# A selective-scan image: which groups take their scan input from VectorE, and how the softplus of a projection is placed

## The chip, the cores and the metric

The kernel runs on one core of one Trainium2 chip. The time is the device time of the program in microseconds (us), the median of several executions. The profile is one execution taken by the hardware profiler. Names used below: PE is TensorE's matrix engine (PEld its weight loads), DVE is VectorE, ACT is ScalarE, POOL is GpSimd, SP is the queue that issues almost all transfers. L564 means line 564 of the kernel before.

## The reference

The input is four images of 384 channels and 32x32 positions. A group normalisation is followed by a selective scan in four directions, a layer norm and a gelu; then causal attention and a mixture of four experts (two used per token). What the change touches is the scan of the first image:

```python
dts = einsum('bkrl,kdr->bkdl', dts, dt_projs_weight)       # rank 12 -> 384 channels
dt = softplus(dts + dt_projs_bias)                          # k = 4 directions
def step(h, inp):
    dtt, ut, bt, ct = inp
    dA = exp(dtt[..., None] * A)                            # A: 16 states per channel
    h = h * dA + (dtt * ut)[..., None] * bt[:, :, None, :]  # the scan, over 1024 positions
    y = einsum('bkdn,bkn->bkd', h, ct)
```

For each image, direction, channel and state there is one linear recurrence over 1024 positions. Its two inputs are the decay `exp(dt * A)`, called `da`, and `v = (dt * u) * B`.

## The kernel before

**Units and groups.** A unit is one [128 x 1024] tile: 32 channels times 4 states on the partitions, 1024 positions along each. There are 768 units, 192 for each image. Four units that share a state quarter `q` and take four channel blocks `j` form a group; one group shares one tile of broadcast B and C rows. The first image has 48 groups, numbered 0 to 47 below. `EACH` is 16 units (one direction k and channel third m), `IMAGE` is 192 units.

**Ticks.** Instructions are issued by hand in a loop over ticks, one tick `t` per unit, and every engine executes its own instructions in that order. Tick `t` issues, in this order: `decay(t+2)` (the exponential `da`, L551, ACT), the multiplication `v = du * B` of unit t (`front`, L558, DVE) unless the unit's v was made another way, `turned(t+1)` (below), the product with C of unit t-1 (`back`, L571, POOL), the scan of unit t (`middle`, L564, DVE), and in the second tick of a group the sum over states of the group before (`row`, L596, PE: eight matmuls, recorded as sixteen). After these come one step of the preparation and the steps of the generators in a list called `side`. A `yield "wait", n` ends a generator's share of this tick and lets it go on n ticks later.

**The second way to v.** In the first image a generator, `feed`, makes v for some groups without DVE. It transposes the rows of `dt * u` on PE into a PSUM bank (L796, two times four 128x128 transposes for a group), multiplies them there by B with 32 ACT instructions of 128x128 (L819, eight in a tick, each eight followed by a wait), and leaves the result in a tile `st`. Then `turned(n)` (L841) transposes eight 128x128 blocks of `st` back, straight into the PSUM tile v of unit n. There are two `st` tiles. A fill may begin when the last but one group begun has been scanned; one that would begin too late (later than `n0 - AHEAD`, with `AHEAD` = 5 ticks) is left out, and the group keeps its DVE multiplication. A group whose v comes this way is called a turned group below, the others plain groups. The loop takes every odd `q`: groups 1, 3, 5 and so on, of which group 1 is left out.

**Buffers.** The PSUM tile v has two buffers, `da` three, h seven. During the first image two PSUM banks are shared by everything else: the projections (`pxd`, L391; `pdt`, L424), the group normalisation, and the transposes of `feed`. A bank is free again when ACT has read it.

**The projections of dt.** `project_dt` runs once for each image, pair of directions and channel third. For each half h of the positions it takes both banks, issues two matmuls (L424), waits a tick, and issues two softplus on ACT (L430). The exponential and the softplus need different ACT tables, so a table load stands before the softplus and another before the next `da`. Ten such projections are issued before tick 192: five of image 0 and five of image 1. The first one of all is made apart (`first_dt`).

Of the kernel before, what the change touches and what calls it, by code (L numbers as in the profile page):

```python
# [33 lines left out]
NQ = N // NI  # L34
NJ = P // DJ
# [7 lines left out]
AHEAD = 5  # L43
# [6 lines left out]
def hybrid_kernel(  # L50
# [60 lines left out]
    clock = [-100]  # L111
# [180 lines left out]
    def columns(v):  # L292

        return v.rearrange("p (h w) -> p w h", w=HW)
# [113 lines left out]
    def project_dt(b, pair, m, u, xd):  # L408

        ks = PAIRS[pair]  # L410
        while not slots.ready(3 + pair):
            yield "wait", 1
        v = u[m]
        if pair == 1:
            v = slots.now(f"ut_{b}_{m}", P, L)
            nc.scalar.copy(v.rearrange("p (w h) -> p w h", h=HW), columns(u[m]))
        dts = [slots.now(f"dt_{b}_{k}_{m}", P, L) for k in ks]
        for h in range(NH):
            while not banks.ready(2):
                yield "wait", 1  # L420
            pss = [banks.now(f"pdt_{b}_{k}_{m}_{h}") for k in ks]
            for i, k in enumerate(ks):
                r = slice(64 * pair + 32 * i, 64 * pair + 32 * i + R)
                nc.tensor.matmul(  # L424
                    pss[i], wdt[r, m * P : (m + 1) * P], xd[r, bass.ts(h, 512)],
                    start=True, stop=True,
                )
            yield "wait", 1
            for i, k in enumerate(ks):
                nc.scalar.activation(  # L430
                    dts[i][:, bass.ts(h, 512)], pss[i], AF.Softplus, bias=dtb[:, k, m : m + 1]
                )
                banks.give(f"pdt_{b}_{k}_{m}_{h}")
        yield "wait", 1
        for i, k in enumerate(ks):
            nc.sync.dma_start(dts_d[b, k][0, m * P : (m + 1) * P, :], dts[i])
            du = yield from slots.take(f"du_{b}_{k}_{m}", P, L)
            nc.vector.tensor_mul(du, dts[i], v)  # L438
            yield "wait", 1
            nc.sync.dma_start(dts_d[b, k][1, m * P : (m + 1) * P, :], du)  # L440
            if b == 0:
                stored_du.add((k, m))
            slots.give(f"dt_{b}_{k}_{m}", f"du_{b}_{k}_{m}")
        if pair == 1:
            slots.give(f"ut_{b}_{m}")

    EACH = NQ * NJ
    IMAGE = M * K * EACH
# [31 lines left out]
    def preparation(b):  # L480

        u = first_x if b == 0 else load_image(b)
        yield "wait", 3
        yield from groupnorm(b, u)
        while clock[0] < IMAGE * (b - 1) + 24:

            yield "wait", 1
        xd = one.tile([P, L], F32, tag="xd", name=f"xd_{b}")
        if b == 0:
            nc.scalar.activation(dump, eps, AF.Softplus)  # L490
            scan_weights()
        yield from project_x(b, 0, u, xd)
        if b == 0:
            fetch(-3, ("bc",))
            first_dt(u, xd)
            yield "start", 0
        yield from project_x(b, 1, u, xd)
        for m in range(M):
            for pair in range(2):
                if b > 0 or m > 0 or pair > 0:  # L500
                    yield from project_dt(b, pair, m, u, xd)
                yield "wait", 0 if b == 0 and m == 0 else 12
# [254 lines left out]
    def feed():  # L757
        bt = one.tile([P, 2, NT, 4 * N], F32, tag="fx0", name="bt")

        def turn_rows(pair):  # L760
            while pair not in stored_rows:
                yield "wait", 1
            rows = yield from slots.take(f"bt_{pair}", 4 * N, L)
            nc.sync.dma_start(rows, rows_d[0, pair].rearrange("k j n l -> (k j n) l"))
            yield "wait", 2
            ps = yield from banks.take(f"pbt_{pair}")
            for t in range(NT):
                nc.tensor.transpose(
                    ps[:, t * 4 * N : (t + 1) * 4 * N], rows[:, t * P : (t + 1) * P],
                    ident[: 4 * N, : 4 * N],  # L770
                )
            yield "wait", 1
            nc.scalar.copy(bt[:, pair], ps.rearrange("p (t n) -> p t n", t=NT))
            banks.give(f"pbt_{pair}")
            slots.give(f"bt_{pair}")

        begun = []
        yield from turn_rows(0)
        for n in range(0, IMAGE, EACH):
            u = units[n]  # L780
            if clock[0] > n + EACH - NJ - AHEAD:
                continue
            if u["pair"] == 1 and u["m"] == 0 and u["i"] == 0:
                yield from turn_rows(1)
            while (u["k"], u["m"]) not in stored_du:
                yield "wait", 1
            name = f"turn_{u['name']}"
            du = yield from slots.take(name, P, L)
            nc.sync.dma_start(du, dts_d[0, u["k"]][1, u["m"] * P : (u["m"] + 1) * P, :])
            yield "wait", 2  # L790

            def dut(q, h, du=du, name=name):
                ps = banks.now(f"{name}_{q}_{h}")
                for t in range(4):
                    o = (4 * h + t) * P
                    nc.tensor.transpose(ps[:, t * P : (t + 1) * P], du[:, o : o + P], ident)  # L796
                return ps

            for q in range(1, NQ, 2):
                n0 = n + q * NJ  # L800
                if clock[0] > n0 - AHEAD:
                    continue
                while len(begun) >= 2 and clock[0] < begun[-2] + NJ:

                    yield "wait", 1
                if clock[0] > n0 - AHEAD:
                    continue
                begun.append(n0)
                st = pools["st"].tile([P, NT, NJ * P], F32, tag="st", name=f"st_{n0}")
                ps = [None, None]  # L810
                for h in range(2):
                    if ps[h] is None:
                        while not banks.ready():
                            yield "wait", 1
                        ps[h] = dut(q, h)
                        yield "wait", 1
                    for t in range(4):
                        for i in range(NI):
                            nc.scalar.activation(  # L819
                                st[:, 4 * h + t, :].rearrange("p (d i) -> p i d", i=NI)[:, i, :],  # L820
                                ps[h][:, t * P : (t + 1) * P], AF.Copy,
                                scale=bt[:, u["pair"], 4 * h + t, u["i"] * 2 * N + q * NI + i :][:, :1],
                            )
                        if t == 1:
                            if h == 0 and banks.ready():
                                ps[1] = dut(q, 1)
                            yield "wait", 1
                    banks.give(f"{name}_{q}_{h}")
                    yield "wait", 1
                scaled[n0] = st  # L830
            slots.give(name)
# [477 lines left out]
    clock[0] = -2  # L1309
    side.append(later())  # L1310
    side.append(feed())
    decay(0)
    decay(1)
# [85 lines left out]
```

## Time and profile before

| | |
|---|---|
| time, median of three runs | 3795.2 us (3794.46 to 3797.17) |
| profiled execution: its time, its span | 3795.0 us, 3793.2 us |
| first image: first scan of image 0 to first scan of image 1 | 49.0 to 680.7 us |
| DVE multiplications for v (L558), all images | 678, mean 1241 ns |
| ACT multiplications by B (L819) | 736, mean 532 ns |
| transposes back to v (L841) | 720, mean 364 ns |
| table loads at the exponential (L551) | 108, mean 1283 ns |
| granted TensorE clock, mean over the span | 0.927 |

The busy times of the profile count instructions from start to end, and consecutive small instructions of one engine overlap, so the mean of 532 ns is not the pace of L819: the timeline, which merges a run of equal instructions, gives the pace. A wait is shown as the idle time ahead of an instruction with the engine and line that ended it.

### The profile page before, as it was taken

The numbers are of one execution on the slowest core, as the hardware profiler recorded it, in microseconds if no ns is written. First come the engines' busy times: TensorE is split into PE (matmuls) and PEld (weight loads), VectorE is DVE, ScalarE is ACT, GpSimd is POOL, SyncE is SP. The second block draws the span as 40 slices with busy tenths as digits, with TensorE's granted clock in tenths as the row PEclk, the third lists the DMA queues.
The fourth block names the chain that finished last, engine by engine and source line by source line (L and its number), as shares of the span: only waits on it lengthen the run. The fifth ranks groups of instructions, "written<-read, shape, count | busy, mean of one in ns | idle before, by whom it ended". The sixth has DMA issues, their size and how long they took to land.

```text
span 3793.2 us, 34275 instructions
## 1 busy us (share of the span) xinstructions
PE 3366.5 (89%) x11543; PEld 1518.3 (40%) x11543; DVE 2964.4 (78%) x2084; ACT 2089.9 (55%) x2767; POOL 1815.1 (48%) x776
## 2 busy tenths in 40 slices
PE   4666666689999999799999999889999999999999
PEld 1333333245333334345333343354343434644444
DVE  6899899998889999989998999999999982210000
ACT  5888888555656656556655555455554552422121
POOL 2777777554455556445555565455665550000000
PEclk7767877799999999898999999899999999999999
DMA  6655655635576767336666565345656551222321
GB/s 207 218 209 219 220 199 208 230 122 184 191 245 208 255 205 251 140 136 225 215 221 223 197 212 185 143 167 195 215 194 237 180 182 38 91 78 80 96 83 53
DMA packets 407983, 678.80 MB, mean 179 GB/s; under 512 B 33488, under 2 KB 280576, under 8 KB 407808
## 3 DMA queue, kind: packets, MB, share of 16 engines
q1 hardware_dynamic: 401600, 676.22, 52.0%
q8 instruction: 91, 1.49, 0.2%
q10 hardware_dynamic: 6208, 0.39, 0.1%
q14 instruction: 84, 0.69, 0.1%
HBM read 604.57 MB, written 71.96 MB: 178 GB/s over the span
## 4 chain that ended last, share of the span: by engine, by line
DVE 42%; PE 40%; ACT 7%; issue 6%; DMA 3%; POOL 1%; DVEq 0%; SPq 0%; POOLq 0%; ACTq 0%
DVE h L564 25%; PE ph L1182 13%; PE fy L1207 13%; DVE v L558 12%; PE y L596 4%; ACT da L551 2%; PE ss L925 2%; PE pq L896 2%; PE pv L907 2%; PE v L841 1%; PE pxd L391 1%; ACT st L819 1%; DVE du L438 1%; DMA du<-dts 1%; PE po L991 1%
## 5 line engine op out<-in xcount | busy, mean ns | idle before, releaser
L571 POOL TENSOR_TENSOR h<-h,bc 128x1024 f32<-128x1024 f32 x768 | 1814.0, 2366 | 1308.6 <-DVE v L558 1142.8
L564 DVE TENSOR_TENSOR_SCAN h<-da,v 128x1024 f32<-128x1024 f32 x768 | 1750.5, 2284 | 104.4 <-PE v L841 29.7
L551 ACT ACTIVATE da<-dt,a 128x1024 f32<-128x1024 f32 x768 | 883.3, 1156 | 923.7 <-DVE h L564 887.2
L1182 PE MATMUL ph<-fx,w 128*128 128x512 f32 x2304 | 1024.8, 601 | 6.5 <-ACT dt L430 2.3
L1207 PE MATMUL fy<-ht,w 128*128 128x512 f32 x2304 | 1021.2, 600 | 1.5 <-ACT dt L430 0.9
L558 DVE TENSOR_TENSOR v<-du,bc 128x1024 f32<-128x1024 f32 x678 | 841.7, 1241 | 38.8 <-DMA du<-dts 21.7
L1182 PEld LDWEIGHTS ph<-fx,w 128*128 128x128 f32 x2304 | 434.9, 192 | 583.4 <-issue 528.9
L1207 PEld LDWEIGHTS fy<-ht,w 128*128 128x128 f32 x2304 | 436.8, 192 | 574.9 <-issue 552.2
L596 PE MATMUL y<-h,sel 128*32 128x512 f32 x3072 | 493.8, 661 | 101.4 <-POOL h L571 101.3
L1167 ACT ACTIVATE ht<-ph,b1s 128x512 f32<-128x512 f32 x384 | 257.2, 678 | 459.5 <-PE ph L1182 459.1
L1216 DVE SCALAR_TENSOR_TENSOR fy<-fy,b2s,tw 128x512 f32<-128x512 f32 x96 | 72.4, 754 | 425.8 <-PE fy L1207 425.8
L596 PEld LDWEIGHTS y<-h,sel 128*32 128x32 f32 x3072 | 97.4, 116 | 412.2 <-issue 219.8
L841 PE MATMUL v<-ident,st 128*128 128x128 f32 x720 | 143.1, 364 | 110.6 <-DVE h L564 110.6
L819 ACT ACTIVATE st<-turn,bt 128x128 f32<-128x128 f32 x736 | 213.6, 532 | 0.1
L841 PEld LDWEIGHTS v<-ident,st 128*128 128x128 f32 x720 | 115.4, 189 | 155.6 <-DVE h L564 78.3
L1171 ACT ACTIVATE ht<-ht 128x3072 f32<-128x3072 f32 x64 | 176.9, 2763 | 0.8
L551 ACT ACT_TABLE_LOAD x108 | 138.6, 1283 | 13.8 <-DMA dt<-dts 11.9
L991 PE MATMUL po<-pt,vt 128*128 128x256 f32 x480 | 105.4, 368 | 9.4 <-ACT pt L887 9.4
L424 PE MATMUL pdt<-xd,wdt 12*128 12x512 f32 x184 | 81.0, 762 | 34.8 <-ACT dt L430 19.4
L925 PE MATMUL ss<-axn,qt 128*128 128x512 f32 (+3 forms) x288 | 106.1, 514 | 0.8 <-ACT pr L943 0.5
L991 PEld LDWEIGHTS po<-pt,vt 128*128 128x128 f32 x480 | 93.1, 195 | 24.9 <-ACT pt L887 12.0
L939 DVE TENSOR_REDUCE nb<-ss 128x1 f32<-128x512 f32 (+3 forms) x48 | 26.1, 554 | 78.8 <-PE ss L930 63.5
(200 smaller groups left out, 1661.7 us busy)
## 6 DMA issues: line engine op xcount, KB each, us to landing
bc<-rows SPq DMA_DIRECT2D x384, 512.0 KB, 4.9
w<-in_w SPq DMA_DIRECT2D x384, 384.0 KB, 6.1
dt<-dts SPq DMA_DIRECT2D x192, 512.0 KB, 3.8
du<-dts SPq DMA_DIRECT2D x192, 512.0 KB, 6.7
dts<-dt SPq DMA_DIRECT2D x48, 512.0 KB, 5.3
dts<-du SPq DMA_DIRECT2D x48, 512.0 KB, 3.8
fx<-t2d SPq DMA_DIRECT2D x12, 768.0 KB, 5.3
tw<-mkd SPq DMA_DIRECT2D x32, 256.0 KB, 6.3
```

The source lines that it names most:

```text
L551: nc.scalar.activation(u["da"], spread["dt4", n], AF.Exp, scale=a4[:, g, u["q"] : u["q"] + 1])
L558: return nc.vector.tensor_tensor(u["v"], spread["du4", n], spread["bc", n][:, 0, :], ALU.mult)
L564: nc.vector.tensor_tensor_scan(u["h"][:, ::step], u["da"][:, ::step], u["v"][:, ::step], 0.0, op0=ALU.mult, op1=ALU.add,)
L571: product = nc.gpsimd.tensor_tensor(h, h, spread["bc", n][:, 1, :], ALU.mult)
L596: nc.tensor.matmul(y, sel, h, start=first, stop=last, tile_position=(0, jj * DJ))
L819: nc.scalar.activation(st[:, 4 * h + t, :].rearrange("p (d i) -> p i d", i=NI)[:, i, :], ps[h][:, t * P : (t + 1) * P], AF.Copy, scale=bt[ ...
L841: nc.tensor.transpose(u["v"][:, t * P : (t + 1) * P], st[:, t, u["j"] * P : (u["j"] + 1) * P], ident)
L925: nc.tensor.matmul(ps[:, : e - o], qt[:, c, i * P : (i + 1) * P], xn[:, c, o:e], start=(c == 0), stop=(c == M - 1 and e <= i * P),)
L991: nc.tensor.matmul(pv[:, o:], vt[:, j, m * P : (m + 1) * P], pts[step][j // 4][:, j % 4, o:], start=False, stop=(j == nj - 1),)
L1167: nc.scalar.activation(ht[:, f, :], ps, AF.Identity, bias=bias)
L1182: nc.tensor.matmul(ps, tiles[n][:, c, (f % 2) * P : (f % 2 + 1) * P], xns[h][:, c, :], start=(c == 0), stop=(c == M - 1),)
L1207: nc.tensor.matmul(pss[m], tiles[n][:, f, :], hts[fh][:, f, :], start=(fh == 0 and f == 0), stop=(fh == 1 and f == FH - 1),)
```

## The change

Two edits. In `project_dt` the tick between the matmuls and the softplus stays for the first half, and goes for the second half while the first image is being scanned: the four softplus of one projection then follow each other in one tick, with the second pair of matmuls between the two pairs of softplus. In `feed` the choice of groups changes from every odd `q` to the groups whose number modulo five is 1, 3 or 4. The rule on late fills and the number of `st` tiles are the same.

```diff
@@ project_dt
             for i, k in enumerate(ks):
                 r = slice(64 * pair + 32 * i, 64 * pair + 32 * i + R)
                 nc.tensor.matmul(
                     pss[i], wdt[r, m * P : (m + 1) * P], xd[r, bass.ts(h, 512)],
                     start=True, stop=True,
                 )
-            yield "wait", 1
+            if h == 0 or clock[0] >= IMAGE:
+
+                yield "wait", 1
             for i, k in enumerate(ks):
                 nc.scalar.activation(
                     dts[i][:, bass.ts(h, 512)], pss[i], AF.Softplus, bias=dtb[:, k, m : m + 1]
                 )
@@ feed
-            for q in range(1, NQ, 2):
+            for q in range(NQ):
                 n0 = n + q * NJ
-                if clock[0] > n0 - AHEAD:
+                if n0 // NJ % 5 not in (1, 3, 4) or clock[0] > n0 - AHEAD:
                     continue
                 while len(begun) >= 2 and clock[0] < begun[-2] + NJ:
 
                     yield "wait", 1
```

In the program that results, 26 groups of the first image are turned: 3, 6, 8, 9, 11, 13, 14, 16, 18, 19, 21, 23, 24, 26, 28, 29, 31, 33, 34, 36, 38, 39, 41, 43, 44 and 46. Before, 23 were: 3 (three of its four units), 5, 7, and every odd group up to 47. The counts of the two programs:

| instruction | before | after |
|---|---|---|
| L558, DVE multiplication for v | 678 | 664 |
| L819, ACT multiplication by B | 736 | 832 |
| L796, transposes of dt * u | 184 | 208 |
| L841, transposes back to v | 720 | 832 |
| table loads at L430 and at L551 | 46 and 108 | 36 and 97 |

SP issues the same number of transfers. From the layer norm of image 1 on, PE has the same instructions in the same order; between tick 192 and there, the preparation of the next images stands a tick or a few earlier.

## The prediction

> **What bounds the kernel now.** I first read the table by stage. Its columns are: the stretch and its length, then busy time of PE, PEld, DVE, ACT and POOL, each with its number of instructions, then the granted TensorE clock, the DMA share and GB/s.
>
> ```profile
> 97.00:216.00 119.00, 77.51 (x347) 36.33 (x345) 108.09 (x59) 98.04 (x214) 85.24 (x36) 0.74 0.59 213
> 216.00:448.00 232.00, 146.92 (x723) 76.11 (x723) 214.29 (x126) 198.67 (x412) 171.81 (x72) 0.76 0.60 219
> 448.00:681.00 233.00, 146.86 (x675) 72.75 (x674) 217.23 (x119) 182.84 (x363) 171.90 (x73) 0.72 0.58 212
> 681.00:1900.00 1219.00, 1121.30 (x3972) 503.21 (x3973) 1121.13 (x811) 737.11 (x819) 652.45 (x277) 0.94 0.58 200
> ```
>
> The first three rows are the first image, the only place that the change edits. DVE is busy 92% there (540 of 584 us), PE 64%, POOL 73%. ACT's 82% overstates it (below). Next I asked the waits between 96 and 680 us who is late:
>
> ```profile
> DVE h L564 <- PE v L841: 29.7, 21, 3.8
> ...
> ACT da L551 <- DVE h L564: 101.1, 82, 3.6
> ```
>
> Columns: total us, times, longest. DVE waits for practically one thing, the transposes that make v in turned groups, 29.7 us. ACT waits 101.1 us for scans to free a `da` buffer: it runs ahead of DVE and is not the limit. Third, DVE's timeline around a clean turned group (15):
>
> ```profile
> 250.54 2.29 DVE L564 TENSOR_TENSOR_SCAN h<-da,v 128x1024 f32<-128x1024 f32 x1
> 252.75 1.29 DVE L558 TENSOR_TENSOR v<-du,bc 128x1024 f32<-128x1024 f32 x1
> 254.17 8.91 DVE L564 TENSOR_TENSOR_SCAN h<-da,v 128x1024 f32<-128x1024 f32 x4
> 263.98 2.29 DVE L564 TENSOR_TENSOR_SCAN h<-da,v 128x1024 f32<-128x1024 f32 x1 [0.91 <-PE v L841]
> ```
>
> A plain unit steps 254.17 - 250.54 = 3.63 us from scan to scan; over all 75 such steps between 97 and 681 us the mean is 3.66. A turned unit without a wait steps 2.20 us. The last unit of the group waits 0.91 us. PE shows why:
>
> ```profile
> 258.69 1.97 PE L841 MATMUL v<-ident,st 128*128 128x128 f32 x8 [0.21 <-DVE h L564]
> 260.59 2.24 PE L596 MATMUL y<-h,sel 128*32 128x512 f32 x16
> 262.75 1.09 PE L841 MATMUL v<-ident,st 128*128 128x128 f32 x8
> ```
>
> With two v buffers the transposes of a unit can start when the scan two units earlier has ended; in the second tick the row (2.24 us) stands between them, and the next v is late.
>
> **Removed: 14 multiplications on DVE.** 678 - 664 = 14 at L558. Each takes its step from 3.66 to 2.20 us: 14 x 1.46 = 20.4 us, all of it on the path, since DVE sets the pace.
>
> **Added on ACT: 3 fills, hidden.** 96 more instructions at L819. Their pace is in ACT's timeline:
>
> ```profile
> 402.43 1.18 ACT L551 ACTIVATE da<-dt,a 128x1024 f32<-128x1024 f32 x1
> 403.45 2.34 ACT L819 ACTIVATE st<-turn,bt 128x128 f32<-128x128 f32 x8
> 405.46 1.24 ACT L551 ACTIVATE da<-dt,a 128x1024 f32<-128x1024 f32 x1
> ```
>
> Eight of them take 405.46 - 403.45 = 2.0 us of the queue, a fill 8.0, three fills 24 us. A tick with eight costs ACT 3.03 us (402.43 to 405.46), less than a plain DVE step, more than a turned one. Before, fills mostly fall into plain groups; now each second group of a pair (9, 14, 19, 24, 29, 34, 39, 44) has the eights in its ticks 1 to 3, where ACT loses 3 x (3.03 - 2.20) = 2.5 us. Its cover is the lead: `da` of unit n+2 starts when scan n-1 ends, takes 1.15, and is wanted two scans (4.4 us) later, a lead of 3.25 us; a plain group, where ACT gains 0.6 to 2.5 us a tick, follows each time. So 0 us; if the cover is gone, up to 2.5 us for each of these eight groups. Here the Trainium skill speaks against the change: "ScalarE: Activation LUTs", section "Rules for kernel authors", puts multiplications on VectorE, as the faster engine for them (its factor is for bf16; all is fp32 here). By the work it is right even here: a unit's v costs ACT 2.0 us (and PE a transpose back) against 1.46 us on DVE. If ACT were the limit, the change would be worth 24 us of fills against the table loads below, about nothing. The row with 101.1 us of ACT waiting decides: I count DVE's side.
>
> **Taken away on ACT: 21 table loads, hidden.** ACT's timeline at a projection:
>
> ```profile
> 419.27 1.28 ACT L430 ACT_TABLE_LOAD   x1
> 420.57 1.26 ACT L430 ACTIVATE dt<-pdt,dtb 128x512 f32<-128x512 f32 x2
> 421.85 1.28 ACT L551 ACT_TABLE_LOAD   x1
> 423.14 1.15 ACT L551 ACTIVATE da<-dt,a 128x1024 f32<-128x1024 f32 x1
> ```
>
> 21 x 1.28 = 27 us, so ACT as a whole is 3 us better off. The skill's page just named, section "What ACT_TABLE_LOAD costs", sets 2.66 us for a switch, a drain of 1.38 included, which would make 56 us; the rows show the next instruction 0.01 to 0.02 us after the load's end, so 1.28 it is. On the path it is worth nothing except through PE, which stands at the second `pdt` until ACT has read the first bank; that wait stays, because the second matmuls still need the banks of the first softplus. New is that ACT waits for them: two short matmuls, of which one lies under a softplus, some 0.5 us in 10 projections, covered by the lead. The four softplus with their loads last 1.28 + 4 x 0.6 + 0.5 + 1.28 = 5.5 us; the lead (3.25) plus one scan (2.2) just covers this in a turned group, and easily in a plain one (7.3 for two steps).
>
> **Added on PE: 112 + 24 transposes, and where they stand.** A further turned unit brings eight transposes (1.04 to 1.97 us over 66 such runs), a tick has 2.20, so they fit as they do now. The transposes of dt * u come in fours, 0.60 to 1.12 us (34 blocks). Before, these stand in plain groups nearly always; in the eight second groups of a pair the fours now stand in ticks 0 and 1. In tick 0 there is room. In tick 1 the four stand behind the row and ahead of the last unit's v: that wait grows by 0.60 to 1.12 us. I take 1.12, as PE is often at the slow pace here (clock 0.72 to 0.76): 8 x 1.12 = 9.0 us.
>
> **Stalls, before and after.** Of the 29.7 us, groups that meet a projection or a normalisation hold most: group 3 has 2.5, group 7 5.2, group 27 6.7, group 33 2.2, group 41 2.1, together 18.7. The other 18 hold 11.0, 0.6 each. Group 27 is the one where a `pxd` waited for a bank that ACT still read, with v behind it:
>
> ```profile
> 411.93 2.84 PE L391 MATMUL pxd<-x,wx 128*128 128x512 f32 x6 [2.38 <-ACT bc L400]
> ...
> 415.78 2.29 DVE L564 TENSOR_TENSOR_SCAN h<-da,v 128x1024 f32<-128x1024 f32 x1 [3.81 <-PE v L841]
> ```
>
> I laid the new order against the ticks. The softplus now fall at ticks 5, 11, 28, 44, 62, 109, 129, 147, 167 and 183. Of these only tick 44 has turned units right behind it (group 11): v of unit 46 waits behind the second `pdt` (ACT: decay 1.05, load 1.28, first softplus 0.6 after scan 43), the transposes for the next fill (which want the bank of the third softplus) and its own eight; about 7 us after scan 43, against two scans of 2.2: 2.5 us, and 1.7 for the row and the second four, 4.2 in all. Group 3 I put at 1.5, group 24 (normalisation) at 1.5, group 26 (`pxd` beside its first units) at 2.0. The other 22 have 0.6 each. After: 22 x 0.6 + 9.0 + 4.2 + 1.5 + 1.5 + 2.0 = 31.4 us, against 29.7: +1.7.
>
> POOL takes 2.37 us a product against 2.20 of a turned step and so falls behind 0.17 a unit, 1.4 over a pair; the waits just counted (0.6 and 1.7) give that back.
>
> **After the first image.** DVE and PE are both at 92% there, and their work is the same but for a few ticks' shift of the preparation, so the gain arrives whole. I allow 3 us either way.
>
> **Sum.** -20.4 + 1.7 = -18.7 us. On the profiled execution (span 3793.2, with 1.8 us around it, 3795.0) that is 3776.3; the median is 0.2 us above that execution, so about 3777 us.
>
> **Rivals.** (1) Half is eaten: the fours wait for banks, or `da` comes late in second groups, up to 2.5 us in most of eight. Then -18.7 + 8 x 1.6 = about -6, 3789. For it: in the waits of before PE already stands 13.5 us at `pdt` for softplus. Against it: a fill takes a bank only when ACT's reads of it stand ahead, and the fill before ended three ticks or so earlier. (2) More than I count: fewer loads also clear the stalls beyond 0.6 that I left in groups 3, 11, 24 and 26 (6.8 us), and the fours run at 0.60 (8 x 0.52 = 4.2 us less): -18.7 - 11.0 = about -30, 3766. For it: the two worst stalls of before (groups 7 and 27) stand beside loads. (3) Slower: in each pair PE's queue head waits for ACT in a turned group, as at 415.78 us, so that one more stall of 3.8 us falls into each of eight pairs: 8 x 3.8 = 30 against 18.7, +12, 3807. It decides from 18.7 / 8 = 2.3 us a pair on. For it: second groups now join fill, row and return transposes on PE. Against it: in ticks 0 and 1 of these groups the banks are free and ACT has its lead. (4) The count is as told by the program itself, so a change without effect is not to be had; but if PE, not DVE, bound the image, the step would stay at 3 us and the time at 3795. PE's 64% and the merged scans of 8.91 us speak against it.
>
> **How the numbers follow.** The likeliest, with its own range of -11 to -25 (3770 to 3784), gets 0.60; rival 1 0.17, rival 2 0.12, rival 3 0.06, rival 4 0.05. A difference under 0.2% (7.6 us) can't be told from none. Faster by more: 0.60 + 0.12 + a third of rival 1 = 0.78. Within: 0.16. Slower: 0.06. The range leaves out the far end of rival 2 and rival 3: 3765 to 3793.
>
> **What would show it.** In the profile after: L558 664 times; the turned step still 2.20; DVE waits for v 28 to 35 us in the first image, with 1.5 to 2 us ahead of the last unit of each second group and about 4 us in group 11; ACT still waiting for scans, at 70 to 110 us; the first scan of image 1 at about 662 us. I am wrong if DVE waits for `da`, if waits in second groups pass 2.3 us beyond those of the others, or if what the first image gains is lost after it.

## The result and the profile after

The changed kernel takes 3787.36 us, the median of 15 runs (3783.72 to 3791.61), against 3795.2 us (3789.45 to 3803.41) for the kernel before, run beside it. The ratio is 0.998, with a 95% interval of 0.9973 to 0.9988. It is faster by 7.8 us where 18.7 were forecast. 3787 lies inside the range (3765 to 3793), but outside the likeliest case's own (3770 to 3784); the number nearest to it is that of the first rival, 3789. A later repeat of the changed kernel (`e11_changed_again`) gave 6.4 us (3790.7 against 3797.12). The profiled execution took 3788.9 us with a span of 3787.2, which is 6.0 less than before.

In the changed kernel, and in all others that keep both edits without new lines above them, the lines behind the first edit stand two lower: the scan is L566, the multiplication L560, `da` L553, the fill L821, the transposes L843, `du` L440, softplus L432.

The page's groups, after (busy us, mean ns of one, then the idle time before them and what ended most of it):

```profile
L566 DVE TENSOR_TENSOR_SCAN h<-da,v 128x1024 f32<-128x1024 f32 x768 | 1749.4, 2284 | 97.6 <-PE v L843 19.8
...
L560 DVE TENSOR_TENSOR v<-du,bc 128x1024 f32<-128x1024 f32 x664 | 825.8, 1244 | 37.2 <-DMA du<-dts 20.2
```

There are 664 multiplications, so the 14 are gone. The table by stage, after, with the same columns as before; the last row ends at the first scan of image 1:

```profile
97.60:221.40 123.80, 82.05 (x370) 39.52 (x370) 112.99 (x62) 93.97 (x207) 86.43 (x37) 0.72 0.63 219
221.40:446.00 224.60, 154.83 (x790) 83.62 (x790) 202.89 (x114) 197.51 (x455) 170.70 (x72) 0.75 0.60 216
446.00:676.50 230.50, 149.69 (x715) 72.62 (x714) 217.62 (x115) 184.83 (x408) 172.47 (x73) 0.76 0.61 223
```

From unit 12 to the first scan of image 1 the image now lasts 578.9 us (583.8 before) and DVE is still busy for 533.5 of them, 92% again. The first scan of image 1 starts at 676.5 us, against 680.7 before and 662 forecast. So most of the gain is missing already inside the first image. The waits of DVE there (60 to 681 us; total, times, longest), after:

```profile
DVE h L566 <- PE v L843: 19.8, 26, 2.4
DVE du L440 <- ACT dt L432: 7.5, 9, 2.0
DVE v L560 <- DMA du<-dts: 5.1, 4, 2.5
```

and those of ACT (49 to 681 us), after:

```profile
ACT da L553 <- DVE h L566: 85.8, 64, 3.7
ACT dt L432 <- PE pdt L424: 19.2, 11, 3.2
```

The wait for the transposes fell from 29.7 to 19.8 us, where I had it rise to 31.4. The second row of DVE has no counterpart before: the multiplication `du = dt * u` (L440, twice for each projection, in the ticks behind the softplus) never waited then. Beside it stands ACT's: the second pair of softplus waits 19.2 us for its matmuls; before, ACT waited 1.1 us for `pdt`.

A book of DVE's time, from the first scan of image 0 to the first scan of image 1, taken from the two traces instruction by instruction (busy time without overlap, us):

| | before | after | difference |
|---|---|---|---|
| length | 631.7 | 626.2 | -5.5 |
| multiplications for v (102, 88), busy | 123.0 | 108.4 | -14.6 |
| idle before multiplications for v | 3.2 | 6.8 | +3.6 |
| scans, busy | 433.3 | 432.1 | -1.2 |
| idle before scans | 44.9 | 33.4 | -11.5 |
| `du` (20), busy | 23.5 | 30.0 | +6.5 |
| idle before `du` | 0 | 7.5 | +7.5 |
| one operation of the normalisation, stretched | 0.5 | 2.7 | +2.2 |
| idle before the normalisation | 0 | 2.1 | +2.1 |

This is one execution of each; in the trace of the repeat the same stretch is 629.1 us long, 2.6 less than before. The 14.0 us at `du` are the largest loss. The timeline after, around the projection at unit 109, shows where it comes from:

```profile
413.05 2.07 PE L424 MATMUL pdt<-xd,wdt 12*128 12x512 f32 x2 [5.02 <-ACT st L821]
...
414.97 1.28 ACT L432 ACT_TABLE_LOAD   x1
415.05 3.64 PE L598 MATMUL y<-h,sel 128*32 128x512 f32 x16
...
416.27 1.27 ACT L432 ACTIVATE dt<-pdt,dtb 128x512 f32<-128x512 f32 x2
...
418.62 2.08 PE L424 MATMUL pdt<-xd,wdt 12*128 12x512 f32 x4
420.73 1.27 ACT L432 ACTIVATE dt<-pdt,dtb 128x512 f32<-128x512 f32 x2 [3.19 <-PE pdt L424]
421.45 1.23 DVE L440 TENSOR_TENSOR du<-dt,x 128x1024 f32<-128x1024 f32 x1 [1.99 <-ACT dt L432]
...
422.02 1.28 ACT L553 ACT_TABLE_LOAD   x1
...
423.31 1.15 ACT L553 ACTIVATE da<-dt,a 128x1024 f32<-128x1024 f32 x1
```

Between the softplus of the first half and those of the second ACT stands 3.19 us: PE has the row sum in its queue (3.64 us), then the second matmuls (2.08 us). From the first load to the next `da` it is 8.3 us instead of the 5.5 in my sum. In six of the ten projections there is no row in between, and the stop is the matmuls alone, 1.58 us, as at unit 44:

```profile
209.63 1.27 ACT L432 ACTIVATE dt<-pdt,dtb 128x512 f32<-128x512 f32 x2 [1.58 <-PE pdt L424]
```

The first line at unit 109 shows a second new wait: a matmul of the first half stands 5.02 us at the head of PE's queue until ACT has read a fill's transposes from the bank that it wants, so the row behind it starts late. Over the first image (60 to 681 us), after:

```profile
PE pdt L424 <- ACT st L821: 16.4, 5, 5.1
```

Before, this wait was 4.5 us, in two times.

### The profile page after: what moved, and what is told of

Read it like the earlier page. It is cut to its first block, busy times and chain, and to the rows that moved or that the text cites. A ratio compares the mean times of both kernels' runs of the same rounds, so it can differ in the third digit from the quotient of the medians.

```text
span 3787.2 us, 34585 instructions
## 1 busy us (share of the span) xinstructions
PE 3382.9 (89%) x11679; PEld 1527.3 (40%) x11679; DVE 2961.2 (78%) x2070; ACT 2085.0 (55%) x2841; POOL 1816.6 (48%) x776
## 4 chain that ended last, share of the span: by engine, by line
DVE 42%; PE 38%; ACT 8%; issue 6%; DMA 3%; POOL 1%; SPq 1%; DVEq 0%; POOLq 0%; ACTq 0%
DVE h L566 25%; PE ph L1184 13%; DVE v L560 13%; PE fy L1209 12%; PE y L598 3%; ACT da L553 2%; PE pq L898 2%; PE pv L909 2%; ACT st L821 2%; POOL h L573 1%; PE pxd L391 1%; PE pdt L424 1%; PE ss L927 1%; DVE fy L1218 1%; PE po L993 1%
## 5 line engine op out<-in xcount | busy, mean ns | idle before, releaser
L573 POOL TENSOR_TENSOR h<-h,bc 128x1024 f32<-128x1024 f32 x768 | 1815.5, 2369 | 1302.8 <-DVE v L560 1071.6
L566 DVE TENSOR_TENSOR_SCAN h<-da,v 128x1024 f32<-128x1024 f32 x768 | 1749.4, 2284 | 97.6 <-PE v L843 19.8
L553 ACT ACTIVATE da<-dt,a 128x1024 f32<-128x1024 f32 x768 | 887.6, 1163 | 891.1 <-DVE h L566 851.7
L560 DVE TENSOR_TENSOR v<-du,bc 128x1024 f32<-128x1024 f32 x664 | 825.8, 1244 | 37.2 <-DMA du<-dts 20.2
L821 ACT ACTIVATE st<-turn,bt 128x128 f32<-128x128 f32 x832 | 244.5, 554 | 0.1
L843 PE MATMUL v<-ident,st 128*128 128x128 f32 x832 | 148.1, 339 | 88.0 <-DVE h L566 87.2
L843 PEld LDWEIGHTS v<-ident,st 128*128 128x128 f32 x832 | 122.0, 176 | 130.1 <-DVE h L566 75.7
L424 PE MATMUL pdt<-xd,wdt 12*128 12x512 f32 x184 | 91.5, 833 | 49.0 <-ACT dt L432 23.6
L553 ACT ACT_TABLE_LOAD x97 | 124.5, 1283 | 13.4 <-DMA dt<-dts 11.8
```

Of the source, the lines that this page charges most:

```text
L553: nc.scalar.activation(u["da"], spread["dt4", n], AF.Exp, scale=a4[:, g, u["q"] : u["q"] + 1])
L560: return nc.vector.tensor_tensor(u["v"], spread["du4", n], spread["bc", n][:, 0, :], ALU.mult)
L566: nc.vector.tensor_tensor_scan(u["h"][:, ::step], u["da"][:, ::step], u["v"][:, ::step], 0.0, op0=ALU.mult, op1=ALU.add,)
L573: product = nc.gpsimd.tensor_tensor(h, h, spread["bc", n][:, 1, :], ALU.mult)
L821: nc.scalar.activation(st[:, 4 * h + t, :].rearrange("p (d i) -> p i d", i=NI)[:, i, :], ps[h][:, t * P : (t + 1) * P], AF.Copy, scale=bt[ ...
L843: nc.tensor.transpose(u["v"][:, t * P : (t + 1) * P], st[:, t, u["j"] * P : (u["j"] + 1) * P], ident)
```

## The experiments

All kernels here compute the whole reference. Two theories stood at the start. Theory A: the missing gain is the lateness of `du` behind four softplus in one tick. Theory B, the rival: it lies in the larger number of turned groups themselves, in their fills and transposes. Later runs ask a third question, theory C: how much it matters in which ticks the softplus fall; its rival, theory D, is that a run of four softplus costs the same wherever it falls. The kernel before had 3796.23 us in the first four runs, 3795.01 in the next four and 3797.12 in the last three.

For the runs I also laid every step from scan to scan of units 12 to 191 against its nominal length (2.205 us for the scan, 1.31 for a multiplication for v, 1.18 for a `du` or output operation; these are the undisturbed lengths of the traces) and summed the excess, "lost time" below, by place: the seven ticks from a projection's softplus on, the normalisation and `pxd`, other ticks of turned and of plain groups.

| lost time, us | projections | each | normalisation | other turned | other plain | sum | turned units |
|---|---|---|---|---|---|---|---|
| before | 14.5 | 1.6 | 9.0 | 13.8 | 7.2 | 44.5 | 90 |
| after | 27.4 | 3.0 | 11.2 | 11.0 | 6.8 | 56.5 | 104 |
| `e11_changed_again` | 26.8 | 3.0 | 13.2 | 12.8 | 7.0 | 59.8 | 104 |
| `e2_softplus_alone` | 29.6 | 3.0 | 9.7 | 11.2 | 4.8 | 55.4 | 92 |
| `e1_groups_alone` | 23.4 | 2.6 | 11.9 | 20.5 | 7.7 | 63.6 | 97 |
| `e3_after_du_later` | 21.3 | 2.4 | 10.8 | 13.3 | 7.2 | 52.6 | 104 |
| `e4_before_du_later` | 15.4 | 1.7 | 10.4 | 19.5 | 5.4 | 50.7 | 90 |
| `e5_softplus_third_tick` | 13.0 | 1.6 | 13.3 | 12.4 | 10.7 | 49.5 | 104 |
| `e6_softplus_row_tick` | 23.6 | 2.6 | 17.0 | 8.2 | 7.1 | 55.9 | 104 |
| `e7_four_groups_fewer` | 22.4 | 2.5 | 10.9 | 11.9 | 7.1 | 52.3 | 88 |
| `e8_du_later_all_images` | 21.9 | 2.4 | 11.8 | 17.8 | 7.6 | 59.1 | 104 |
| `e9_ticks_held` | 18.5 | 2.1 | 12.8 | 12.9 | 10.5 | 54.7 | 104 |
| `e10_ticks_held_du_later` | 20.7 | 2.3 | 14.4 | 11.7 | 12.4 | 59.2 | 104 |

Before, group 9 like group 3 has only three turned units, hence 90. The changed kernel's repeat shows how far two executions differ: 3.3 us in the sum, 0.6 at the projections. From before to after the sum rises by 12.0 us (15.3 in the repeat), and the projections by 12.9 (12.3). Not held fixed is the granted TensorE clock: over the first image its mean lies between 0.70 and 0.75 in these traces (before and after 0.73 each), and the three longest first images (640.6 to 642.7 us) have 0.70 to 0.72. Which is cause there and which effect is open.

**The softplus edit alone.** The choice of groups is as before.

```diff
-            for q in range(NQ):
+            for q in range(1, NQ, 2):
                 n0 = n + q * NJ
-                if n0 // NJ % 5 not in (1, 3, 4) or clock[0] > n0 - AHEAD:
+                if clock[0] > n0 - AHEAD:
```

> The kernel before with the softplus edit alone (odd q as before). 92 turned units instead of 90, one more projection before tick 192. Theory A: VectorE waits for ACT at du, 7 to 9 us, plus 5 to 7 us of stretched du; against it some 5 to 10 us fewer waits for v: 3791 to 3802. Theory B: no loss from du that matters, fewer table loads: 3784 to 3792.

It took 3802.86 us (3797.78 to 3805.84), 1.0018 (1.001 to 1.0026): 6.6 us slower than the kernel before, though two more units are turned and 23 table loads fewer stand at softplus and `da`. ACT's waits (49 to 681 us) in this run:

```profile
ACT da L553 <- DVE h L566: 101.1, 102, 3.7
ACT dt L432 <- PE pdt L424: 12.3, 13, 3.1
```

ACT's wait for the second matmuls is there without the new groups, and each projection loses 3.0 us instead of 1.6; the wait of `pdt` for a fill's bank is not there at all. Ten projections instead of nine are counted here, in other ticks than before; the sum of lost time rises by 10.9 us. So the edit that I had costed at nothing is enough to make a loss of this size.

**The groups alone.** The wait between the halves is back. The steps of the preparation follow each other at 10 ticks instead of 12 in the first image; with 12, image 0 would not have been ready when image 1 needs its buffers.

```diff
-            if h == 0 or clock[0] >= IMAGE:
-
-                yield "wait", 1
+            yield "wait", 1
...
-                yield "wait", 0 if b == 0 and m == 0 else 12
+                yield "wait", 0 if b == 0 and m == 0 else 10 if clock[0] < IMAGE else 12
```

> The changed choice of groups with the softplus as before (two and two). The pause between projections is two ticks shorter in the first image, since image 0 would otherwise not be ready in time for image 1; banks are held a tick longer, so only 97 units are turned instead of 104. 7 multiplications fewer than before are worth 7 x 1.46 = 10 us. Theory A: du does not wait, the 10 us arrive: 3783 to 3788, as fast as the changed kernel with half as many units moved. Theory B: fills in turned groups take back half or more: 3789 to 3795.

It took 3812.77 us (3809.42 to 3813.52), 1.0042 (1.003 to 1.0055): 16.5 us slower, which neither theory had. With split softplus only 97 of units 12 to 191 are turned, seven more than before. Its waits of DVE (60 to 681 us):

```profile
DVE h L564 <- PE v L841: 35.5, 28, 3.2
DVE h L564 <- POOL h L571: 6.8, 5, 2.8
```

The seven are worth some 9 us (7 x 1.31); against them stand 8.9 more lost at projections, 6.7 more in other turned ticks, and 7 behind the first image. So the two edits don't add up: 6.6 and 16.5 us slower apart, 7.8 faster together. Only with the grouped softplus are all groups of the new choice filled in time (104 turned units against 97). Why the split form loses so much in ticks without a projection is not settled; the pause differs too, and with it the ticks of the projections, so this run is no clean test of B.

**`du` one tick later.** To test A directly, `du` is issued a tick later, when the softplus are done; the preparation's pause is one shorter, so that the rest keeps its ticks.

```diff
-        yield "wait", 1
+        yield "wait", 2 if clock[0] < IMAGE else 1
...
-                yield "wait", 0 if b == 0 and m == 0 else 12
+                yield "wait", 0 if b == 0 and m == 0 else 11 if clock[0] < IMAGE else 12
```

> The changed kernel, with the VectorE multiplication du = dt * u (L440) of each first-image projection issued one tick later (two ticks behind the four softplus instead of one; the pause between projections is one tick shorter, so that every projection, fill and turned group keeps its tick). Theory A (du stands in VectorE's queue before ACT has finished the longer run of four softplus, so VectorE waits 7.5 us and is stretched by 6.5 us, and the transfers behind late stores cost some more): the waits of L440 for ACT fall from 7.5 to under 1 us, its 20 durations in the first image from 30.0 to about 24 us, the first image from 626 to about 613 us, the time to 3772 to 3778. Theory B (the fills in turned groups slow ACT and PE, whatever du does): the time stays within 3 us of 3787.

The waits at `du` are gone, and `du` is busy for 23.5 us again as before, but the time is 3789.59 us (3782.74 to 3792.11), 0.998 (0.9971 to 0.9988), the ratio of the changed kernel. The profiled execution is its fastest run, with a first image of 620.4 us; the others don't bear that out. Part of the wait moved: `DVE h L566 <- PE v` is 27.5 us here, 19.8 in the changed kernel. The same place in both, the projection at unit 44. DVE's timeline of the changed kernel:

```profile
207.18 2.29 DVE L566 TENSOR_TENSOR_SCAN h<-da,v 128x1024 f32<-128x1024 f32 x1 [0.72 <-POOL h L573]
210.35 2.63 DVE L440 TENSOR_TENSOR du<-dt,x 128x1024 f32<-128x1024 f32 x1 [0.89 <-ACT dt L432]
213.30 2.29 DVE L566 TENSOR_TENSOR_SCAN h<-da,v 128x1024 f32<-128x1024 f32 x1 [0.32 <-PE v L843]
215.50 1.20 DVE L440 TENSOR_TENSOR du<-dt,x 128x1024 f32<-128x1024 f32 x1
217.83 2.29 DVE L566 TENSOR_TENSOR_SCAN h<-da,v 128x1024 f32<-128x1024 f32 x1 [1.12 <-PE v L843]
220.03 1.21 DVE L560 TENSOR_TENSOR v<-du,bc 128x1024 f32<-128x1024 f32 x1
221.37 2.29 DVE L566 TENSOR_TENSOR_SCAN h<-da,v 128x1024 f32<-128x1024 f32 x1
```

and with `du` a tick later:

```profile
202.69 2.29 DVE L566 TENSOR_TENSOR_SCAN h<-da,v 128x1024 f32<-128x1024 f32 x1 [0.72 <-POOL h L573]
208.84 2.29 DVE L566 TENSOR_TENSOR_SCAN h<-da,v 128x1024 f32<-128x1024 f32 x1 [3.86 <-PE v L843]
211.04 1.20 DVE L440 TENSOR_TENSOR du<-dt,x 128x1024 f32<-128x1024 f32 x1
212.16 2.28 DVE L566 TENSOR_TENSOR_SCAN h<-da,v 128x1024 f32<-128x1024 f32 x1
214.36 1.20 DVE L440 TENSOR_TENSOR du<-dt,x 128x1024 f32<-128x1024 f32 x1
215.48 1.22 DVE L560 TENSOR_TENSOR v<-du,bc 128x1024 f32<-128x1024 f32 x1
216.83 2.29 DVE L566 TENSOR_TENSOR_SCAN h<-da,v 128x1024 f32<-128x1024 f32 x1
```

The same work, three scans with two `du` and one multiplication, takes 221.37 - 207.18 = 14.19 us and 216.83 - 202.69 = 14.14 us. One wait of 3.86 us for v stands for 0.89 + 0.32 + 1.12 us of waits and a `du` stretched by 1.4. Behind the softplus not only `du` is late, but also the second matmuls on PE and the transposes of v that are queued behind them. So A falls as the cause; `du` is where the delay shows.

**The same on the kernel before**, as a control. Against the changed kernel:

```diff
-            if h == 0 or clock[0] >= IMAGE:
-
-                yield "wait", 1
+            yield "wait", 1
...
-        yield "wait", 1
+        yield "wait", 2 if clock[0] < IMAGE else 1
...
-                yield "wait", 0 if b == 0 and m == 0 else 12
+                yield "wait", 0 if b == 0 and m == 0 else 11 if clock[0] < IMAGE else 12
...
-            for q in range(NQ):
+            for q in range(1, NQ, 2):
...
-                if n0 // NJ % 5 not in (1, 3, 4) or clock[0] > n0 - AHEAD:
+                if clock[0] > n0 - AHEAD:
```

> The kernel before with the same move alone: du one tick later, everything else in its tick. A control. Theory A: nothing to gain, because du of the kernel before never waited for ACT (0 us): within 3 us of 3795. If a later du is worth something by itself (fewer clashes with GpSimd's products), up to 3 us faster, and this has to be taken off what the run before it shows.

3800.97 us (3796.4 to 3806.15), 1.0013 (1.0006 to 1.0019): 4.7 us slower. Where `du` never waited, moving it gains nothing.

**`du` later in all images.**

```diff
-        yield "wait", 1
+        yield "wait", 2
...
-                yield "wait", 0 if b == 0 and m == 0 else 12
+                yield "wait", 0 if b == 0 and m == 0 else 11
```

> The changed kernel with du two ticks behind the last softplus in all four images (the pause between projections one tick shorter). In the trace of the changed kernel VectorE stands 31 us before du between tick 192 and the last scan. If VectorE sets the end there, 10 to 25 us of that are won: 3762 to 3777. If PE or ACT does, the wait moves to the next v or to the matrix engine: 3783 to 3790, as with the move in the first image alone.

3784.74 us (3781.15 to 3791.94), 0.9975 (0.9967 to 0.9983): the interval overlaps that of the changed kernel, and the 10 to 25 us hoped for are not there. DVE's wait for v in the first image is 32.0 us here: it moves on again.

**Other ticks for the softplus.** In the changed kernel the softplus fall on ticks 11, 28, 44, 62, 109, 129, 147, 167 and 183. Here the start of a projection in the first image is held to chosen places of the pattern of 20 ticks that the choice of groups makes. First, softplus in every twentieth tick from 22 on:

```diff
-            while not banks.ready(2):
+            while not banks.ready(2) or (
+                h == 0 and 8 < clock[0] < IMAGE and (clock[0] + 1) % 20 not in (7, 8, 2)
+            ):
...
-                yield "wait", 0 if b == 0 and m == 0 else 12
+                yield "wait", 0 if b == 0 and m == 0 else 4 if clock[0] < IMAGE else 12
```

> The changed kernel with the same 26 turned groups, but every projection after the second tick group starts only so that its four softplus fall in tick 2 of a span of 20 ticks (the third tick of the first plain group: no row on PE ahead of the second pdt, two more plain units behind). Nine projections instead of ten stand before tick 192. Theory C (the loss is where the four softplus fall: ACT stands at the second pdt, PE's queue and du stand behind ACT): lost time around projections falls from 27 us to under 12, first image about 610 us, time 3768 to 3778. Theory D (each run of four softplus costs its 3 us wherever it falls): 3784 to 3791.

The first image is 616.5 us long, against 626.2, and the projections lose 13.0 us, 1.6 each as before. Yet the time is 3792.75 us (3789.97 to 3796.7), 0.9998 (0.9989 to 1.0006). The first image ends 15.2 us ahead of the kernel before and unit 288 starts 21.9 ahead, but unit 384 only 4.0. DVE's waits between these two units (1102 to 1508 us):

```profile
DVE du L442 <- ACT dt L434: 19.8, 3, 8.8
```

In the changed kernel the same stretch has 2.0 us of it, and 6.5 us in which `du` waits for PE; the difference, 11.3 us, is the larger part of the 17.9 lost. With the earlier projections the later ones moved too (193, 210, 256 and on instead of 199, 244, 262), to ticks in which ACT is not done with the softplus when `du` comes up. The gain of one image was lost in the next.

Second, softplus in tick 9 of the twenty (tick 11 the first time), beside the row:

```diff
-                h == 0 and 8 < clock[0] < IMAGE and (clock[0] + 1) % 20 not in (7, 8, 2)
+                h == 0 and 8 < clock[0] < IMAGE and (clock[0] + 1) % 20 not in (9, 10, 11)
```

> The same with the softplus in tick 9 of 20, the second tick of the other plain group, in which the row of the group before (2 to 3.6 us of PE) stands ahead of the second pdt. Ten projections before tick 192, the same 26 turned groups. Theory C: ACT waits about 3 us at each second pdt, VectorE 2 us at each du; about 4 us lost at each projection, 35 to 42 in all instead of 27: 3794 to 3804. Theory D: 3784 to 3791.

3792.49 us (3790.79 to 3800.56), 0.9998 (0.999 to 1.0007); the first image 624.9 us, 23.6 lost at the projections. I had thought the row's tick the worst place; it is not worse than the ticks of the changed kernel. Later projections moved here as well.

**The price of a turned unit.** Groups 19, 29, 34 and 39, all second groups of pairs, keep their DVE multiplication; the projections are held to the ticks of the changed kernel.

```diff
-            while not banks.ready(2):
+            while not banks.ready(2) or (
+                h == 0 and 12 < clock[0] < IMAGE
+                and clock[0] + 1 not in (28, 44, 62, 109, 129, 147, 167, 183)
+            ):
...
-                yield "wait", 0 if b == 0 and m == 0 else 12
+                yield "wait", 0 if b == 0 and m == 0 else 4 if clock[0] < IMAGE else 12
...
-                if n0 // NJ % 5 not in (1, 3, 4) or clock[0] > n0 - AHEAD:
+                if n0 // NJ % 5 not in (1, 3, 4) or n0 // NJ in (19, 29, 34, 39) or clock[0] > n0 - AHEAD:
```

> The changed kernel without four of its turned groups (19, 29, 34, 39, each the second of a pair with no projection in it); the projections are held to the ticks they have in the changed kernel. 16 multiplications come back to VectorE, three of them more than the change had moved away. If a moved unit is worth the 1.46 us of the prediction less the wait of such a group (0.2 us as measured): 16 x 1.46 - 1 = 22 us slower, 3806 to 3813. If moved units are worth only about half (the reading that the gain of 18.7 came to 7.8 because of them): about 10 us slower, 3795 to 3801.

3807.72 us (3801.55 to 3810.32), 1.0038 (1.0024 to 1.0053), 12.7 us slower than the kernel before. To the changed kernel it is 20.4 us by the medians, 0.0058 x 3795 = 22.0 by the ratios; to its repeat 17.0 and 20.1. That makes 1.06 to 1.38 us for each of 16 units. By the prediction's steps the four groups were worth 16 x 1.46 - 4 x 1.12 - 4 x 0.6 = 16.5 us. Inside the first image the traces show less: it lasts 642.7 us here, 626.2 and 629.1 in the changed kernel and its repeat, so 0.85 to 1.03 us a unit. The rest falls behind it (3117.5 us from the first scan of image 1 to the end, against 3110.7 and 3108.6), where the edit changes nothing that I could name. So B falls as the whole cause: a second group brings the larger part of what its multiplications cost. But it has a share: in the same ticks the projections lose 22.4 us here, 27.4 and 26.8 with the four groups.

**Softplus on better ticks, all later ones held.** The softplus fall in ticks 5, 11, 22, 42, 62, 102, 122, 142, 162 and 182; the projections from tick 198 on have the ticks of the changed kernel.

```diff
-            while not banks.ready(2):
+            while not banks.ready(2) or (
+                h == 0 and 8 < clock[0] < 198
+                and clock[0] + 1 not in (11, 22, 42, 62, 102, 103, 104, 107, 108, 109, 122, 142, 162, 182)
+            ):
...
-                yield "wait", 0 if b == 0 and m == 0 else 12
+                yield "wait", 0 if b == 0 and m == 0 else 4 if clock[0] < IMAGE else 12
```

> The changed kernel with its 26 turned groups and every projection of images 1 to 3 behind tick 192 in the tick it has there; only the ten projections of the first image are moved, to softplus ticks 5, 11, 22, 42, 62, 102, 122, 142, 162 and 182 (all from 22 on in tick 2 of 20). Theory C (place of the softplus): from the places measured so far, lost time around projections 18 us instead of 27, first image about 617 us, and, as nothing behind tick 192 is moved, the gain arrives at the end: 3775 to 3781. If the end of the kernel does not follow the first image even so: 3784 to 3790.

3783.28 us (3782.24 to 3785.41), 0.9964 (0.9951 to 0.9976), the fastest version here by its median, though a little slower than forecast. On the same chip the changed kernel ran again, with no edit:

> The changed kernel itself, once more, on the same chip as the two above, for their comparison: 3784 to 3791.

3790.7 us (3787.02 to 3795.04), 0.9985 (0.9978 to 0.9991). The two spreads don't meet; the difference is 7.4 us. The traces place it only in part. The projections lose 18.5 us against 26.8, but other waits of DVE in the first image rose (60 to 681 us), in the kernel with held ticks:

```profile
DVE h L569 <- PE v L846: 22.6, 22, 3.2
DVE v L563 <- DMA bc<-rows: 8.3, 4, 4.0
DVE v L563 <- DMA du<-dts: 5.6, 4, 2.4
DVE du L443 <- ACT dt L435: 2.0, 2, 1.7
```

By the spans (3780.4 and 3788.3 us) it is 7.9 us faster: 2.3 before the first scan, where no edit reaches, 3.3 in the first image, 2.3 behind it. Nothing is lost behind the first image this time. But the first image, forecast at about 617 us, is 625.8 us long (626.2 and 629.1 in the changed kernel), and the sum of lost time is 54.7 against 56.5 and 59.8: what the projections win is in large part lost again elsewhere in the image. So the version is faster, and theory C explains it only in part.

Last, the same with `du` a tick later in all images; against the kernel with held ticks:

```diff
-        yield "wait", 1
+        yield "wait", 2
...
-                yield "wait", 0 if b == 0 and m == 0 else 4 if clock[0] < IMAGE else 12
+                yield "wait", 0 if b == 0 and m == 0 else 3 if clock[0] < IMAGE else 11
```

> The same with du one tick later in all images (pauses a tick shorter). If du in VectorE's queue is a cost of its own beside the place: 3 to 6 us faster than the run before it, 3770 to 3777. If the wait only moves on to the next v: within 3 us of the run before it.

3785.07 us (3782.98 to 3787.47), 0.9969 (0.9957 to 0.9982): no further gain, as when the wait only moves on to the next v.

## Why the prediction was wrong in size

**What bounds the kernel: right.** DVE is at 92% in the first image before and after, ACT still waits 85.8 us for scans (70 to 110 forecast), and a turned step without a wait is still 2.20 us.

**14 multiplications, 20.4 us: right in kind, somewhat large.** At the undisturbed 1.31 us of DVE they are 18.3 us. By the run with four groups fewer they are worth 14 x 1.06 to 14 x 1.38 = 14.9 to 19.3 by the times, and 12 to 14 inside the first image.

**3 fills, 0 us: right for `da`.** No scan of the first image waits for `da` after (1.1 us before), though the second groups carry the eights. What the prediction weighed against multiplying on ACT did not decide: ACT still waits 85.8 us for scans. But the fills also hold banks, and the projections' matmuls wait for these (16.4 us against 4.5); that was not in the sum.

**Transposes and stalls, +1.7 us: wrong in sign, and small.** The 9.0 us for fours in second groups did not come: in six of the eight the last unit waits 0.24 us, as in group 19:

```profile
312.98 2.29 DVE L566 TENSOR_TENSOR_SCAN h<-da,v 128x1024 f32<-128x1024 f32 x1 [0.24 <-PE v L843]
```

The fours do stand where I put them, between the row and the last unit's eight, but PE was fast: from 308.44 us on, eight transposes, the row, the four and eight more take 1.09, 1.92, 0.66 and 1.04 us, about two scans together. DVE's waits for v fell by 9.9 us. At group 11 the total came out, in part by luck: 0.72 + 0.32 + 1.12 us ahead of its scans and 0.89 ahead of its `du` are 3.05 against 4.2, but only 1.44 of it is for v. And the reading that only tick 44 has turned units right behind it was wrong: group 3 (units 12 to 15) stands behind tick 11 and group 46 (184 to 187) behind tick 183. The projection at unit 11 loses most of all, 5.2 us (6.3 in the repeat); group 3 was priced at 1.5.

**Taken away on ACT, 0 us: the step that failed.** "New is that ACT waits for them: two short matmuls, of which one lies under a softplus, some 0.5 us in 10 projections, covered by the lead." ACT waits 19.2 us in 11 times, not 5: PE takes 2.08 to 2.65 us for the pair (at 418.62 us, and at 44's projection), and with the row ahead of them 3.19 us pass. And the cover that I named, the lead of `da`, covers only `da`. What else waits behind the four softplus was left out: `du` on DVE in the next tick, the engine that sets the pace, and the transposes of v behind the second matmuls on PE. In the trace before, with a tick between the halves, `du` does not wait. The price at the projections is 3.0 us each instead of 1.6, 12.9 in nine. For units 12 to 191 the 18.3 us of multiplications gone and the 12.0 of added lost time make -6.3; the first image measured -5.5 (-2.6 in the repeat), the medians -7.8. The lost time is itself the excess over the nominal lengths, so this sum places the loss; it does not test it.

How this splits between the two edits can't be said with one number. Each alone raises the price of a projection (3.0 and 2.6 us), and together it is 3.0. That the place of the softplus matters is shown by the runs with other ticks (1.6, 2.1, 2.6 and 3.0 us a projection with the same groups and grouped softplus; 1.6, 1.7, 2.1 and 2.8 without the costly projection at tick 11, which the first of them doesn't have). What makes a place good is not shown: the same tick of the twenty costs 0.5 us at unit 182 and 4.3 at unit 42 in the run with held ticks. That ACT's stop for the second matmuls is the start of the delay is read from the timelines and from the softplus edit alone; a kernel with the matmuls of both halves ahead of the softplus, which would take four banks, was not tried. Nor was one in which a fill cannot hold a projection's bank.

**After the first image, 0 plus or minus 3: right for the changed kernel** (4.2 us ahead at unit 192, 6.0 at the end), but not as a rule. One run lost 17.9 us there.

**The rivals.** Rival 1 has the size, but not by its mechanism: `da` came late nowhere, and the last unit of six of the eight second groups waits 0.24 us. Rival 3's mechanism, PE's head of the queue waiting for ACT, is there at projections (`pdt` waits for ACT in the banks), but not in each pair: a price of 3.8 us or more was met four times (5.2, 4.9, 4.2 and 4.3 us of lost time at the projections of units 11, 44, 109 and 129), twice in the repeat (6.3 and 4.0 at 11 and 44), and not eight times.

## What to carry to other kernels

When instructions of one engine are drawn together into one run, list what is queued behind that run on every other engine in the next tick, and price each, above all what stands on the engine that sets the pace; a lead measured for one consumer covers only that consumer. A wait that vanishes after a reorder has often only moved: compare the time of the same work across the place, as with 14.19 and 14.14 us, not the row of the wait. And hold the schedule behind the edited stage fixed when a stage is tuned, or its gain may be lost where nobody looks.

## What the runs showed of the hardware

`du` takes 1.19 to 1.27 us undisturbed, but up to 3.36 us where it starts while POOL is inside a product. The timeline after, DVE and POOL at the projection of unit 11:

```profile
95.43 4.46 DVE L566 TENSOR_TENSOR_SCAN h<-da,v 128x1024 f32<-128x1024 f32 x2
95.47 6.99 POOL L573 TENSOR_TENSOR h<-h,bc 128x1024 f32<-128x1024 f32 x3 [1.26 <-DVE v L560]
...
100.18 3.35 DVE L440 TENSOR_TENSOR du<-dt,x 128x1024 f32<-128x1024 f32 x1 [0.29 <-ACT dt L432]
```

POOL's third product ends at 95.47 + 6.99 = 102.46, and `du` at 103.53, 1.07 us later: it did its work after the product, as if it had stood still till then. At 210.35 us it is the same (POOL ends at 211.90, `du` at 212.98, 1.08 later). The Trainium skill has this ("SBUF — State Buffer", section "SBUF: two separate sides"): the two engines share a pair of ports under an exclusive lock, and of a VectorE operation with two SBUF inputs and a GpSimd operation that reads SBUF, the one that starts first holds it for the whole instruction. The trace agrees, with 6.5 us over 20 `du`. Where `du` follows its scan at once, POOL's product has begun with that scan and is nearly over (2.35 us against 2.2). Where `du` has to wait for the softplus, it depends on the next unit. If that is turned, POOL may begin the product of the scan just ended first, and `du` then waits for that too: so a wait of 0.29 us here cost 0.29 + 3.35 - 1.23 = 2.4. If it is plain, the kernel holds that product back until DVE has made the unit's v (`POOL h L573 <- DVE v L560`: 131.7 us, 81 times, 60 to 681 us), which stands behind `du` in DVE's queue, and `du` keeps its 1.23 us even after a wait of 1.99 (at 421.45 us). All nine waits of the changed kernel fall so: three before a turned unit (ticks 12, 45 and 184, `du` 3.35, 2.63 and 3.36 us), six before a plain one (1.23 us each). The third:

```profile
649.41 3.36 DVE L440 TENSOR_TENSOR du<-dt,x 128x1024 f32<-128x1024 f32 x1 [0.28 <-ACT dt L432]
```

So one way in which the two edits meet is shown: the grouped softplus make `du` wait, and the turned units let POOL go ahead of it. The three make up 5.7 of the 6.5 us by which `du` grew; with `du` a tick later all of it was gone, and the kernel's time was the same.
